# Edge rows added behind the column sums, and a third tile of re-read rows skipped by a branch

## The chip, the cores and the metric

The kernel runs on one core of one Trainium2 chip. The metric is the device time of that core in microseconds (us). Three runs of the kernel before gave a median of 324.0 us (323.58 to 324.59).

## What is computed

```python
N, d = feat.shape                      # 16384 rows of 256
q, k, v = feat @ Wq, feat @ Wk, feat @ Wv
starts = jnp.searchsorted(bids, jnp.arange(B))       # B = 8
pos = jnp.arange(N) - starts[bids]
qp, kp, vp = (pad(q), pad(k), pad(v))  # .at[bids, pos].set, LMAX = 3072 places each
scores = where(mask, einsum('bld,bmd->blm', qp, kp), NEG)
rp = einsum('blm,bmd->bld', softmax(scores), vp)
r = rp[bids, pos]
t = r @ Wt
mu, var = t.mean(axis=0), t.var(axis=0)
tn = (t - mu) / jnp.sqrt(var + EPS) * gamma + beta
return feat + relu(tn)
```

The segment numbers `bids` of the input are not sorted. So `pos` of many rows lies outside 0 to 3071. A row that is written to a place of its segment is an own row of it (436, 511, 542, 726, 701, 698, 431 and 468 rows in the eight segments). Rows whose `pos` runs past an end of the segment read the row at that end when results are fetched: these are the edge rows, two for each segment, 16 in all, and thousands of outputs use them. A further group of 199 rows writes a place that a later row overwrites, and reads back the other row's result: the kernel calls them losers, and keeps them in up to three tiles of 128 rows (LT = 3), the third of which is empty for this input.

The batch normalization at the end needs the sum and the sum of squares of each column over all 16384 rows of t, and then a scale and a shift for each column.

## The kernel before, in words

The kernel writes its instructions for five engines itself: TensorE (PE), VectorE (DVE), ScalarE (ACT), GpSimd (POOL) and SyncE (SP). A helper class records each operation (`op`, line 588), finds the operations that it depends on, and makes the engine wait on semaphores for them. Each engine runs its own operations in the order in which the code records them. Nothing reorders them later. So the order in the source text is the order on each engine.

The first part sorts the rows by segment. For each of eight segments e, POOL gathers the own rows into `xs`, in up to six tiles of 128 (FT = 6). PE and ACT form queries, keys and values, the scores and the exponentials. `attend(e, u)` (line 1273) multiplies the exponentials of tile u by the values on PE and takes a reciprocal on DVE; `scale` (line 1293) makes the result tile in `tk` and, after tiles 3 and 5, stores it to the table `t_rows` in device memory through SP's queue. Each result tile is then squared on ACT (`square`) and added to `acc` on DVE (`moments`, line 1337, two operations a tile), weighted by how often each row is read as an own row. In the last segment the tiles come in the order 0, 1, 4, 5, 2, 3.

The edge rows of the first seven segments are gathered from `t_rows` into `ecat` (line 1751). Edge rows that lie in the last segment are picked out of `tk` by small selection matmuls into `b_e`, a bank of PSUM: tiles 0, 4, 5 and 1 at line 1781, added to `ecat` at line 1786, squared at line 1787; tiles 2 and 3 at lines 1873 to 1875, added at line 1892 for the output alone (their share of the sums is in the weights `rw`).

Two matmuls close the column sums in the PSUM tile `sums`: one weighs the 16 edge rows and their squares (`we`, line 1876), one adds up the partitions of `acc` (line 1877). DVE transposes `sums` into `st_t` (line 1884), makes mean, variance, scale and shift, and transposes them back into `ss`.

The second part writes the output in 16 groups of 1024 rows. For a group, PE adds the edge row that each row reads (through the 0/1 matrices `hot`) into PSUM, and in some groups the input rows too (`open_group`). DVE (or ACT) brings the sum to the buffer `f`, and SP stores it. SP also loads the input rows for later groups, and counts each store that has landed in a semaphore `done`. Between the groups DVE normalizes the result tiles of one segment each (`normal`, `normal_more`). When a segment's groups have been stored, POOL scatters its tiles to their rows of the output, one indirect DMA for each 128 rows (`put`), because these rows must overwrite what the groups wrote. Behind the eight segments it scatters the three tiles `tl` of losers (line 2029). Tiles 4 and 5 of a segment are skipped by a branch where the segment has no such rows (line 2022). Last, POOL waits until all scatters have landed (a semaphore against a count in a register, loaded at line 1865) and all engines are through.

Of the kernel before, what the change touches and what calls it, by code (L numbers as in the profile page):

```python
# [11 lines left out]
I32 = mybir.dt.int32  # L12
BF16 = mybir.dt.bfloat16
F16 = mybir.dt.float16
AF = mybir.ActivationFunctionType
ALU = mybir.AluOpType
# [4 lines left out]
P = 128  # L21
NB = 8
# [8 lines left out]
LT = 3  # L31
# [870 lines left out]
def fast_path(nc, feat, bids, wq, wk, wv, wt, gamma, beta, out, bad):  # L902
    N, D = feat.shape
# [5 lines left out]
    NG = J // GT  # L909
    NL = NB + 1  # L910
    TT = NB * FT
    QA, QB = 4 * P, 2 * P
    pg = Fast(nc)

    room = ExitStack()
    start = nc._sbuf_addr_for_side("left")
# [9 lines left out]
    def new(name, shape, dtype=F32):  # L926
        nonlocal end
        size = mybir.dt.size(dtype)
        for d in shape[1:]:
            size *= d  # L930
        plan.append((name, shape, dtype, end))
        h = at(name, shape, dtype, end)
        end += size + -size % 32
        return h
# [30 lines left out]
    acc = new("acc", [P, 2, D])  # L965
# [4 lines left out]
    ecat = new("ecat", [P, 2, D])  # L970
# [17 lines left out]
    eidx, ridl, idxo = new("eidx", [P, 1], I32), new("ridl", [P, LT], I32), new("idxo", [P, LT], I32)  # L988
    eps_t = new("eps_t", [P, 1])
    armf, arm = new("armf", [1, NB]), new("arm", [1, NB], I32)  # L990
    upto, order = new("upto", [1, NB + 2], I32), new("order", [1, NG], I32)
    gb = new("gb", [P, 2, 32])
    gt_, bt_ = gb[:, 0, 0:NB], gb[:, 1, 0:NB]
    mq, ss8 = new("mq", [P, 2, NB]), new("ss8", [P, 2, NB])
# [75 lines left out]
    def load(eng, key, ap, hi, lo=0):  # L1070
        def emit(e):
            regs[key] = e.value_load(ap, min_val=lo, max_val=hi)

        pg.op(eng, emit, [ap], [], bare=True)
# [651 lines left out]
    for e in range(NB):  # L1726
# [18 lines left out]
        if last:  # L1745
            for u in (0, 1, 4, 5, 2, 3):
                step(e, u)
                if u == 0:
                    scores(e, 1, range(4))
                    late[2]()  # L1750
                    pg.gather(ecat[:, 0, :], t_rows[0 : (NB - 1) * FW, :], eidx[:], (NB - 1) * FW)
                    for g in range(FIRST, EARLY):
                        load_group(g)
                if u == 1:
                    scores(e, 1, range(4, 6))
                    late[4]()
                if u == 4:
                    late[3]()
                if u == 0:
                    lag[:0] = [(NB, t) for t in range(LT)]  # L1760
                if u == 5:
                    first = square(e, 1)
                    for g in range(EARLY, MID):
                        load_group(g)
                if u == 1:
                    pg.act(row_sum[:], ones[:], AF.Identity, scale=reads_r[:, e * FT + 1 : e * FT + 2])
                if u == 3:
                    any_ = hot[0 : 2 * NB, 0:2, :, :].rearrange("p k u x -> p (k u x)")
                    pg.mm(sums[:], none[0 : 2 * NB, :], any_, start=True, stop=False)
                    by_row(row_sum, first[0], first[2])  # L1770
                if u == 3:
                    while lag or squared:
                        if lag and len(squared) < 2:
                            squared.append(square(*lag.pop(0)))
                        else:
                            moments()
                else:
                    past(e)
                if u == 2:
                    b_e = ps_s[0]  # L1780
                    for u_ in (0, 4, 5, 1):
                        pg.mm(
                            b_e[:, 0:D], sel[:, u_, :], tk[:, e * FT + u_, :], start=(u_ == 0), stop=(u_ == 1),
                            pred=over4(e, u_),
                        )
                    pg.tt(ecat[:, 0, :], ecat[:, 0, :], b_e[:, 0:D], ALU.add)
                    pg.act(ecat[:, 1, :], ecat[:, 0, :], AF.Square)
        else:
            busy = e + 2 < NB
            step(e, 0, lambda: (xt_main(n, 0), xt_main(n, 1)))  # L1790
# [52 lines left out]
            if e == NB - 4:  # L1843
                prefix(NB - 1, NB)
                sizes(NB - 1)
                pg.copy("DVE", armf[:], arm[:])
                pg.red(cnt_f[0:1, 0:1], armf[:])
                pg.ts(upto[:, NB + 1 : NB + 2], cnt_f[0:1, 0:1], 16.0, ALU.mult, 16.0 * (4 * NB + LT), ALU.add)
                todo, late = rows()
                work.extend(todo)  # L1850
            scores(n, 0, range(4, 6))
# [2 lines left out]
            slot()  # L1854
        if last:
            assert not lag and not squared
        pg.end_region()
        if e == NB - 2:
            slot(99)
# [2 lines left out]
        load("POOL", ("g", e_), upto[0:1, e_ : e_ + 1], NG, 1)  # L1862
    for e_ in range(NB):
        load("POOL", ("t", e_), arm[0:1, e_ : e_ + 1], 2)
    load("POOL", "rows", upto[:, NB + 1 : NB + 2], 16 * (TT + LT), 16 * (4 * NB + LT))

    for g in range(MID, NF):
        load_group(g)
# [4 lines left out]
    b_e = ps_s[3]  # L1873
    for x, m in enumerate(last_two):
        pg.mm(b_e[:, 0:D], sel[:, 2 + x, :], tk[:, m, :], start=(x == 0), stop=(x == 1))
    pg.mm(sums[:], we[:], ecat[0 : 2 * NB, :, :].rearrange("p s d -> p (s d)"), start=False, stop=False)
    pg.mm(sums[:], ones[:], acc[:].rearrange("p s d -> p (s d)"), start=False, stop=True)
    pg.ts(good[:], rdens[:], LIM, ALU.is_lt)
    pg.stt(good[:], rdens[:], 1.0 / LIM, good[:], ALU.is_gt, ALU.mult, accum=odd[:])
    pg.ts(odd[:], odd[:], -1.0, ALU.mult, float(TT), ALU.add)  # L1880
# [145 lines left out]
            pg.op("POOL", emit, [idx[:, m : m + 1]], [])  # L2026
    look("POOL")
    pg.op("POOL", lambda x: (x.wait_ge(done, 1), x.wait_ge(done, regs[("g", NB)])), [], [])
    for t in range(LT):
        pg.put(out, idx[:, TT + t : TT + t + 1], tl[:, t, :], N)  # L2030

    held = pg.run("rows")
    held += [done, *row_done]
# [54 lines left out]
```

## Time and profile before

| | |
|---|---|
| median of three runs | 324.0 us |
| the profiled execution | 323.04 us |
| its span, first to last instruction | 318.4 us |
| busy: PE, DVE, ACT, POOL | 249.3, 238.8, 150.3, 133.8 us |
| mean granted TensorE clock | 0.866 |
| DMA over the span | 52.49 MB, 165 GB/s; 333 to 418 GB/s in most of the last third |
| chain that ended last, by engine | PE 41%, DVE 26%, ACT 11%, issue 9%, POOL 6%, DMA 4% |

The profile is of one execution. Times in it count from the span's start. A line of the chain or of a timeline gives the start, the duration, the engine, the line of code (often that of a helper: L803 is every matmul, L842 every scalar_tensor_tensor, L894 every unconditional scatter), and what is written from what. In brackets stands how long the engine was idle before it, and what ended that. A busy share is an average over the span; what a stage waits for is read from the stage's own lines. The sums are complete at 231.9 us, so the first part takes about 232 us and the second 86 us.

### The profile page before, as it was taken

What the parts mean: (1) busy time and instruction counts of PE and PEld (TensorE: products, weight loads), DVE (VectorE), ACT (ScalarE), POOL (GpSimd) and SP (SyncE); (2) the same over time, 40 slices, a digit from 0 to 9 for tenths busy, and PEclk for the clock granted to TensorE, in tenths of its full rate; (3) what the DMA queues carried; (4) which work ended last, traced back from release to release, by engine and by line L of the source; (5) the groups of instructions that cost most, each with busy time, mean ns of one, the idle gap of its engine ahead of it and who ended that gap; (6) DMA issues with size and microseconds to landing.
All of it is one profiled execution on the core that took longest, in us unless ns stands there. A gap on an engine that the chain in (4) does not pass through costs nothing.

```text
span 318.4 us, 4632 instructions
## 1 busy us (share of the span) xinstructions
PE 249.3 (78%) x1279; PEld 162.2 (51%) x1279; DVE 238.8 (75%) x773; ACT 150.3 (47%) x294; POOL 133.8 (42%) x143
## 2 busy tenths in 40 slices
PE   4699779998999999989999999859776955642600
PEld 2465547675676777667766777547322322210200
DVE  4845759988669576748776889866679999999930
ACT  3126949884764485255736557749501221111000
POOL 7433307051071034223502463776040337787873
PEclk9559979999999999999999999997965897775555
DMA  3101104114047014210300135198997999998795
GB/s 104 35 23 28 40 2 129 52 54 141 6 87 169 1 29 126 97 31 19 106 33 3 33 104 165 20 333 342 337 402 300 372 398 418 415 414 342 311 374 199
DMA packets 21533, 52.49 MB, mean 165 GB/s; under 512 B 5488, under 2 KB 14786, under 8 KB 17530
## 3 DMA queue, kind: packets, MB, share of 16 engines
q1 hardware_dynamic: 15674, 41.37, 34.6%
q0 software_dynamic: 5280, 10.18, 11.0%
q10 hardware_dynamic: 544, 0.52, 0.5%
q8 instruction: 15, 0.25, 0.3%
q14 instruction: 20, 0.16, 0.2%
HBM read 26.27 MB, written 28.74 MB: 173 GB/s over the span
## 4 chain that ended last, share of the span: by engine, by line
PE 41%; DVE 26%; ACT 11%; issue 9%; POOL 6%; DMA 4%; another core or an unknown queue 1%; POOLq 1%; DVEq 0%; SPq 0%
PE ps L803 39%; DVE tk L822 6%; DVE f L822 5%; POOL out L894 4%; ACT pa L813 4%; ACT xT L813 2%; PE ps L808 2%; DMA ecat<-t_rows,eidx 2%; ACT vs L818 2%; DMA t_rows<-tk 2%; DVE junk L829 2%; DVE k L819 1%; DVE tk L1942 1%; DVE tk L1944 1%; ACT xs L818 1%
## 5 line engine op out<-in xcount | busy, mean ns | idle before, releaser
L878 POOL DMA_INDIRECT xs<-in_r_feat,idx x48 | 50.8, 1059 | 100.3 <-DVE idx L842 52.0
L803 PE MATMUL ps<-vs,pa 128*128 128x257 f32 x312 | 78.0, 394 | 7.2 <-ACT vs L818 3.8
L803 PEld LDWEIGHTS ps<-vs,pa 128*128 128x128 f32 x312 | 57.9, 194 | 20.7 <-issue 7.5
L894 POOL DMA_INDIRECT out<-tk,idx x32 | 34.4, 1075 | 28.4 <-DVE tk L842 19.2
L803 PE MATMUL ps<-wvt,xT 128*128 128x256 f32 x156 | 37.5, 386 | 1.5 <-ACT vs L818 0.7
L818 ACT COPY f<-ps 128x1024 f32<-128x1024 f32 (+1 forms) x12 | 9.8, 835 | 58.7 <-PE ps L803 56.1
L803 PE MATMUL ps<-y,hot 32*128 32x256 bf16 x256 | 14.3, 353 | 26.5 <-DVE f L822 16.8
L803 PEld LDWEIGHTS ps<-wvt,xT 128*128 128x128 f32 x156 | 28.8, 190 | 11.3 <-ACT sq L813 2.3
L813 ACT ACTIVATE pa<-ps,mask 128x512 f32<-128x512 f32 x48 | 29.5, 687 | 10.6 <-PE ps L803 9.3
L803 PE MATMUL ps<-f,ident 128*128 128x512 f32 x38 | 29.0, 893 | 1.7 <-DVE f L822 1.2
L803 PEld LDWEIGHTS ps<-y,hot 32*128 32x128 bf16 x256 | 6.5, 111 | 43.6 <-DVE f L822 25.2
L822 DVE TENSOR_TENSOR f<-f,ps 128x1024 f32<-128x1024 f32 (+3 forms) x17 | 26.0, 1559 | 3.5 <-remote 2.9
L819 DVE COPY k<-ps 32x128 f32<-32x128 f32 x48 | 14.1, 294 | 17.5 <-PE ps L803 16.7
L818 ACT COPY vs<-ps 128x512 f32<-128x512 f32 x24 | 14.2, 590 | 25.2 <-PE ps L803 16.6
L813 ACT ACTIVATE q<-ps,cqk 96x512 f32<-96x512 f32 (+3 forms) x32 | 18.4, 573 | 13.6 <-PE ps L803 13.2
L855 DVE RECIPROCAL rdens<-ps 128x1 f32<-128x1 f32 x48 | 7.7, 160 | 22.6 <-PE ps L803 22.6
L803 PE MATMUL ps<-xT,w 128*128 128x512 f32 (+1 forms) x48 | 22.4, 593 | 2.3 <-ACT xT L813 2.3
L813 ACT ACTIVATE xT<-ps,negx 128x512 f32<-128x512 f32 (+1 forms) x32 | 17.0, 586 | 15.2 <-PE ps L808 9.8
L842 DVE SCALAR_TENSOR_TENSOR acc<-tk,reads_r,acc 128x256 f32<-128x256 f32 x45 | 21.4, 477 | 1.5 <-issue 1.3
L842 DVE SCALAR_TENSOR_TENSOR acc<-sq,reads_r,acc 128x256 f32<-128x256 f32 x45 | 21.5, 477 | 0.3 <-ACT sq L813 0.3
L878 POOL DMA_INDIRECT reads_r<-reads_of,idx x12 | 12.0, 1003 | 23.0 <-DVE ge L831 11.7
L813 ACT ACTIVATE pb<-ps,mask 128x256 f32<-128x256 f32 x48 | 19.3, 483 | 4.0 <-PE ps L803 3.8
(271 smaller groups left out, 426.2 us busy)
## 6 DMA issues: line engine op xcount, KB each, us to landing
f<-in_r_feat SPq DMA_DIRECT2D x16, 1024.0 KB, 7.7
out<-f SPq DMA_DIRECT2D x15, 1024.0 KB
t_rows<-tk SPq DMA_DIRECT2D x8, 512.0 KB, 4.2
t_rows<-tk SPq DMA_DIRECT2D x8, 256.0 KB, 2.2
eb<-edge_of SPq DMA_DIRECT2D x16, 64.0 KB
out<-f SPq DMA_DIRECT2D x2, 512.0 KB, 2.7
xs<-in_r_feat,idx POOLq DMA_INDIRECT x48, 3.6
out<-tk,idx POOLq DMA_INDIRECT x39
```

What stands on the lines that cost most here:

```text
L803: "PE", lambda e: e.matmul(out, lhsT, rhs, start=start, stop=stop, skip_group_check=True),
L808: return self.op("PE", lambda e: e.transpose(out, in_, ident), [in_, ident], [out], pred=pred)
L813: "ACT", lambda e: e.activation(out, in_, func, bias=bias, scale=scale), [in_, *more], [out]
L818: return self.op("ACT", lambda e: e.copy(out, in_), [in_], [out])
L819: return self.op(eng, lambda e: e.tensor_copy(out, in_), [in_], [out])
L822: return self.op(eng, lambda e: e.tensor_tensor(out, a, b, op), [a, b], [out])
L829: lambda e: e.tensor_scalar(out, a, s1, s2, op0, op1, accum_out=accum)
L842: else e.scalar_tensor_tensor(out, a, s, b, op0, op1),
L855: return self.op("DVE", lambda e: e.reciprocal(out, in_), [in_], [out])
L878: lambda e: e.indirect_dma_start(out=out, out_offset=None, in_=table, in_offset=bass.IndirectOffsetOnAxis(ap=ind, axis=0), bounds_check=n ...
L894: lambda e: e.indirect_dma_start(out=table, out_offset=bass.IndirectOffsetOnAxis(ap=ind, axis=0), in_=src, in_offset=None, bounds_check=n ...
L1942: v.tensor_tensor(y, y, scale, ALU.mult).then_inc(sem, 1)
```

## The change

Three things change. The add and the square of `ecat` move from behind the selection matmuls of tile 2 to the end of the last segment's loop, behind all operations that fill `acc`. The two matmuls that close `sums` change places. And the last of the three tiles of losers is scattered only if more than 256 rows are losers: DVE forms that flag and corrects the count of scatters to wait for (two more operations of one element each), POOL loads the flag into a register, and a branch passes over the scatter if it is 0.

```diff
-    upto, order = new("upto", [1, NB + 2], I32), new("order", [1, NG], I32)
+    upto, order = new("upto", [1, NB + 3], I32), new("order", [1, NG], I32)
...
                             pred=over4(e, u_),
                         )
-                    pg.tt(ecat[:, 0, :], ecat[:, 0, :], b_e[:, 0:D], ALU.add)
-                    pg.act(ecat[:, 1, :], ecat[:, 0, :], AF.Square)
...
                 pg.red(cnt_f[0:1, 0:1], armf[:])
-                pg.ts(upto[:, NB + 1 : NB + 2], cnt_f[0:1, 0:1], 16.0, ALU.mult, 16.0 * (4 * NB + LT), ALU.add)
+                lost = n_bc[0:1, NB : NB + 1]
+                pg.ts(upto[:, NB + 2 : NB + 3], lost, (LT - 1.0) * P, ALU.is_gt)
+                pg.stt(cnt_f[0:1, 0:1], lost, (LT - 1.0) * P, cnt_f[0:1, 0:1], ALU.is_gt, ALU.add)
+                pg.ts(upto[:, NB + 1 : NB + 2], cnt_f[0:1, 0:1], 16.0, ALU.mult, 16.0 * (4 * NB + LT - 1), ALU.add)
...
         if last:
             assert not lag and not squared
+            pg.tt(ecat[:, 0, :], ecat[:, 0, :], b_e[:, 0:D], ALU.add)
+            pg.act(ecat[:, 1, :], ecat[:, 0, :], AF.Square)
...
-    load("POOL", "rows", upto[:, NB + 1 : NB + 2], 16 * (TT + LT), 16 * (4 * NB + LT))
+    load("POOL", "rows", upto[:, NB + 1 : NB + 2], 16 * (TT + LT), 16 * (4 * NB + LT - 1))
+    load("POOL", "lost", upto[:, NB + 2 : NB + 3], 1)
...
-    pg.mm(sums[:], we[:], ecat[0 : 2 * NB, :, :].rearrange("p s d -> p (s d)"), start=False, stop=False)
-    pg.mm(sums[:], ones[:], acc[:].rearrange("p s d -> p (s d)"), start=False, stop=True)
+    pg.mm(sums[:], ones[:], acc[:].rearrange("p s d -> p (s d)"), start=False, stop=False)
+    pg.mm(sums[:], we[:], ecat[0 : 2 * NB, :, :].rearrange("p s d -> p (s d)"), start=False, stop=True)
...
-    for t in range(LT):
+    for t in range(LT - 1):
         pg.put(out, idx[:, TT + t : TT + t + 1], tl[:, t, :], N)
+
+    def put_last(x):
+        with x.If(regs["lost"] > 0):
+            pg.put_now(x, out, idx[:, TT + LT - 1 : TT + LT], tl[:, LT - 1, :], N)
+
+    pg.op("POOL", put_last, [idx[:, TT + LT - 1 : TT + LT], tl[:, LT - 1, :]], [])
```

## The prediction

> **What bounds the kernel now.** I read the chain of work that ended last, in order of time, because only what stands on it can shorten the span; then the timelines of DVE, PE and POOL around the two places that the change touches; then busy time by stretches; then the queue's own waits. The chain just ahead of the second half:
>
> ```profile
> 219.79 6.85 DMA ecat<-t_rows,eidx
> 226.66 0.43 DVE ecat L822
> 227.12 0.42 ACT ecat L813
> 227.54 0.37 ACT tk L813
> ...
> 227.95 3.94 PE ps L803 x6
> 231.91 0.73 DVE st_t L858
> ```
>
> The gather of the 16 edge rows lands at 226.66, and the in-order DVE stands in front of it. Behind DVE everything stops, as its timeline shows:
>
> ```profile
> 224.24 0.48 DVE L842 SCALAR_TENSOR_TENSOR acc<-sq,reads_r,acc 128x256 f32<-128x256 f32 x1
> 226.66 0.42 DVE L822 TENSOR_TENSOR ecat<-ecat,ps 128x256 f32<-128x256 f32 x1 [1.95 <-DMA ecat<-t_rows,eidx]
> 227.00 0.16 DVE L855 RECIPROCAL rdens<-ps 128x1 f32<-128x1 f32 x1
> ```
>
> and that of PE:
>
> ```profile
> 227.95 0.70 PE L803 MATMUL ps<-tk,sel 128*128 128x256 f32 x2 [1.96 <-ACT tk L813]
> 228.58 1.29 PE L803 MATMUL ps<-ecat,we 16*128 16x512 f32 x2
> 229.80 2.07 PE L803 MATMUL ps<-acc,ones 128*128 128x512 f32 x2
> ```
>
> The reciprocal at 227.00 belongs to the last attend, whose PE work ended at 224.2: it has nothing to do with the edge rows. From 231.91 (sums complete) DVE works through 239.15 to 299.4 almost without a gap, so the sums start the second half.
>
> The end of the chain is POOL, one scatter per 0.98 us busy plus 0.30 between:
>
> ```profile
> 310.52 0.98 POOL L894 DMA_INDIRECT out<-tl,idx  x1 [0.30 <-issue]
> 311.80 0.99 POOL L894 DMA_INDIRECT out<-tl,idx  x1 [0.30 <-issue]
> 313.10 0.98 POOL L894 DMA_INDIRECT out<-tl,idx  x1 [0.30 <-issue]
> ```
>
> In the trace's landing records the last scatter lands at 317.2, after which POOL closes (drain, clearing of semaphores) until 318.4. A second chain ends close by: SP's last counted store.
>
> ```profile
> L1953 SPq EVENT_SEMAPHORE x16: 17/17/28, 244.5 to 316.4; - x16
> ```
>
> POOL waits for both. So the end is bound by POOL with SP only 0.8 us behind.
>
> **Step 1: the ecat add leaves DVE's place ahead of the reciprocal.** In the new order DVE goes from the acc at 224.24 straight to the reciprocal. Neighbours in this run start 0.40 apart: 224.64. From its start to the end of the six acc operations behind it took 227.00 to 229.53 = 2.53, so acc is complete at 227.17 (it was 229.53). ACT must keep up: tk needs the reciprocal (224.80) and ACT, which is in a square until 225.18; tk 225.1 to 225.6, its square to 226.1; the sixth acc wants that at 226.7. It holds. The selection matmuls of the last tile follow the earlier ones on PE without the 1.96 gap, 225.84 to 226.3.
>
> The add itself now stands behind the six: start 227.1, and the data has been there since 226.66, so it waits for nothing; +0.42, ACT's Square to 227.97. Two edits of order follow: Square now stands behind tk and its square on ACT (no one waits), and ahead of ACT's table load (1.28 at 228.42), which then ends near 229.3; the Sqrt that needs it comes at about 231.2. Hidden, with 1.9 us of cover. The small DVE operations behind the add (good, odd, cnt_f, 0.7 together) end near 228.3, before the sums. Hidden.
>
> **Step 2: acc's matmul goes first, ecat's last.** acc can start at 227.2. Its price depends on PE's clock. The two passes of ecat in the trace started 0.53 apart (228.58, 229.11) at full clock, those of acc 1.01 apart (229.80, 230.81) at half; all are 512 columns. At full clock: 227.21 + 1.06 + 1.06 + 0.2 for the last pass to drain = 229.5; the ecat Square (227.97) is there when its turn comes at 228.27. At half clock: 227.21 + 2.02 + 2.02 + 0.2 = 231.45. Against 231.89 that is a gain of 2.3 or of 0.4.
>
> Which? Rows of the same trace, busy time by stretches (PE busy is the second number, PEclk the granted clock):
>
> ```profile
> 226.00:229.40 3.40, 1.45 (x4) 0.59 (x4) 2.73 (x8) 2.17 (x4) 0.00 (x0) 1.00 0.83 313
> 229.40:232.80 3.40, 3.40 (x6) 1.60 (x6) 1.52 (x8) 0.31 (x1) 0.00 (x0) 0.50 0.97 348
> 256.80:260.20 3.40, 2.48 (x20) 0.91 (x18) 3.33 (x3) 1.75 (x2) 0.00 (x0) 1.00 0.99 384
> ```
>
> A stretch with PE busy 1.45 of 3.4 (43%) was followed by half clock, one with 2.48 (73%) by full (1.00 from 260.2 to 263.5). In the new order PE idles only from 226.3 to 227.2, 0.9 of such a stretch: 73 to 74% busy. [...]
>
> Behind the sums one thing may be lost again: PE finishes the two early group matmuls sooner and may idle nearly 3 us until y is ready, so the 32 short matmuls ahead of the first group add (at full clock in the trace, from 236.2) can fall to half. Sixteen such took 0.61 at full and 1.04 at half, so the loss is 0 to 0.43. I take 0.4: gain at the first group add 2.3 - 0.4 = 1.9.
>
> **Step 3: does 1.9 us live to the end?** DVE is continuous from there, so its part moves along. POOL's first four scatters wait for DVE; the second four (260.88) in truth wait for SP's count of landed stores: DVE's second tk was done at 255.5, the fifth count came at 260.0. From there POOL is continuous. Store landings go over DMA engines that are full for a long time (DMA share is the number before GB/s):
>
> ```profile
> 239.00:245.00 6.00, 2.97 (x53) 1.24 (x41) 5.85 (x5) 1.07 (x2) 0.00 (x0) 0.55 0.68 272
> 245.00:291.00 46.00, 29.64 (x176) 10.54 (x176) 45.01 (x52) 7.80 (x9) 27.95 (x25) 0.76 1.00 400
> 291.00:301.00 10.00, 4.09 (x34) 1.40 (x34) 9.80 (x8) 0.36 (x1) 7.87 (x8) 0.50 0.74 288
> ```
>
> A full server can finish earlier only by closing earlier idle time: 32% of 6 us = 1.9 us lies between 239 and 245, and about 0.8 us between 223 and 232, where the t_rows store and three feat loads behind tk also issue some 2.3 us sooner. Together 2.7 us, more than 1.9. And from 291 to 301 the engines are at 0.74, so the last stores are paced by DVE again. I carry 1.9 through; the bounds are 0 and 2.3.
>
> **Step 4: the third scatter goes.** The segments lose 199 rows by the input's definition, under 256, so the branch is not taken. POOL ends 1.29 us earlier: last landing 317.2 - 1.3 = 315.9. SP's store (316.4) now comes last: of 1.29 only 0.8 counts. The skipped branch: between the scatters at 264.99 and 266.27 lie two branches not taken, and the gap is the 0.30 of all others; cost 0 to 0.15, taken as 0. The register load that feeds it is one more on POOL's sequencer; POOL waits 12.0 us there for t_rows. Two added one-element DVE operations (0.13 to 0.16 each, at 164.4): DVE idles 1.44 at 167.7 for PE, which waits for ACT; hidden, 0.3 if not. The sum of both parts: 1.9 + 0.8 = 2.7. The profiled execution took 323.0 (span 318.4, 4.6 around it): 320.3. The median of before is 324.0, 1.0 above it: 321.3.
>
> **The rivals.** *Clock at half* for acc and ecat: step 2 gives 0.4, with 0.8 of the scatter 1.2: 322.8. For it: the 73% is one example. Chance 0.14. *DMA absorbs it*: store landings hardly move, POOL's second four start where they did; only the scatter and some tenths remain: 323.1. For it: share 1.00 over 46 us. Against: the 2.7 us of idle ahead of it. Chance 0.14, on the line between faster and same. *Slower*: the earlier loads and stores crowd the DMA queue so that the fifth store lands later than before. It took 8.05 us from issue to count (251.97 to 260.02). POOL's 38 scatters behind that count have no slack; beyond the 1.3 of the scatter every further us moves the end, so it decides from a landing at 261.3; at 262.6 the end would be 1.3 later than before, 325.3. Against: the order of the queue is unchanged. Chance 0.10. That the branch does not skip would leave 1.9 and cost 0.8: 322.1, inside the range.
>
> **Numbers.** Forecast 0.62, alone 320.4 to 322.2. Faster by over 0.3% (about 1 us, what a measurement of this kernel can tell from no change): 0.62 + 0.14 + 0.05 = 0.81; same 0.09; slower 0.10. The range 320.2 to 323.6 leaves out the slower case and little else.
>
> **What would show it.** Reciprocal directly behind acc near 224.7 with no wait on ecat; acc's matmul before ecat's, passes 0.53 apart; sums read near 229.6; first group add near 237.3; POOL's second four near 259; two tl scatters; end within 1.3 of SP's last count. Wrong: acc's passes 1.01 apart (step 2), a gather that lands after 227.4 (the ecat matmul then waits), group adds earlier but POOL's second four still at 260.9 (step 3), or a pause like the unexplained 2.85 us ahead of DVE's last group add (306.16, "remote") in a new place.

## The result, and the profile after

| | before | after |
|---|---|---|
| median of 20 runs | 323.92 us (322.15 to 325.63) | 321.44 us (320.29 to 324.75) |
| the profiled execution | 323.04 us | 321.24 us |
| its span | 318.4 us | 316.4 us |
| reciprocal of the last attend | 227.00 | 224.80 |
| `acc` complete | 229.53 | 227.32 |
| sums read by DVE | 231.91 | 229.59 |
| first group add | 239.15 | 236.87 |
| POOL's fifth scatter of the half | 260.88 | 259.44 |
| last scatter issued, seen landed | 313.10, 317.21 | 310.94, 315.25 |
| SP's last counted store | 316.36 | 314.26 |

The ratio is 0.9942 with an interval of 0.992 to 0.9965, which is 1.9 us (1.1 to 2.6); the two medians lie 2.5 apart. Executions more than 1.5% above the fastest of their kernel are left out of all ratios here, not of the medians, and since the profiles of the branch alone and of the swap alone, further down, are of such executions, only their stretch up to the sums is read. The marks are in us from the start of the span of one profiled execution each.

The chain that ended last, around the sums, in order of time (start, duration, engine and what is written). The DMA and the `ecat` add are gone from it; it goes from DVE's last operations on `acc` straight to four PE passes:

```profile
226.44 0.88 DVE acc L842 x2
227.37 2.19 PE ps L803 x4
229.59 0.73 DVE st_t L858
```

DVE's timeline of the changed kernel at the same place. The reciprocal stands 0.40 behind the `acc` operation ahead of it, and no line has a bracket, so nothing is waited for. The add at 227.24 comes 0.5 behind the landing of the gather (226.74 here, from 219.89):

```profile
224.40 0.48 DVE L842 SCALAR_TENSOR_TENSOR acc<-sq,reads_r,acc 128x256 f32<-128x256 f32 x1
224.80 0.16 DVE L855 RECIPROCAL rdens<-ps 128x1 f32<-128x1 f32 x1
...
226.84 0.48 DVE L842 SCALAR_TENSOR_TENSOR acc<-sq,rw,acc 128x256 f32<-128x256 f32 x1
227.24 0.41 DVE L822 TENSOR_TENSOR ecat<-ecat,ps 128x256 f32<-128x256 f32 x1
```

PE's timeline. The idle gap shrank to 0.79, and the two passes of `acc` take 1.13 together where they took 2.07:

```profile
225.56 1.03 PE L803 MATMUL ps<-tk,sel 128*128 128x256 f32 x4
227.37 1.13 PE L803 MATMUL ps<-acc,ones 128*128 128x512 f32 x2 [0.79 <-DVE acc L842]
228.43 1.12 PE L803 MATMUL ps<-ecat,we 16*128 16x512 f32 x2
```

Busy time by stretches (the second number is PE busy, PEclk the granted clock, then the DMA share and GB/s). The clock is 1.00 in both stretches around the sums. The DMA engines, 0.68 busy in the six microseconds behind the first group add of before, are full in the like six of after:

```profile
226.00:229.40 3.40, 2.61 (x7) 0.77 (x5) 2.19 (x10) 1.91 (x3) 0.00 (x0) 1.00 0.90 233
229.40:232.80 3.40, 2.52 (x7) 0.82 (x6) 2.90 (x11) 0.30 (x1) 0.00 (x0) 1.00 1.01 389
...
236.90:242.90 6.00, 3.40 (x49) 1.42 (x42) 6.00 (x5) 1.17 (x2) 0.89 (x1) 0.50 1.00 409
```

POOL's timeline, at the start of the half and at its end. The fifth scatter now names SP's count as its releaser; two scatters of `tl` are left, with the same 0.30 between all:

```profile
253.33 0.98 POOL L894 DMA_INDIRECT out<-tk,idx  x1 [0.31 <-issue]
259.44 0.98 POOL L894 DMA_INDIRECT out<-tk,idx  x1 [5.13 <-SPq L1957]
260.73 1.72 POOL L894 DMA_INDIRECT out<-tk,idx  x1 [0.30 <-issue]
...
309.65 0.98 POOL L894 DMA_INDIRECT out<-tl,idx  x1 [0.30 <-issue]
310.94 0.99 POOL L894 DMA_INDIRECT out<-tl,idx  x1 [0.30 <-issue]
```

And SP's counted stores, the last at 314.3:

```profile
L1957 SPq EVENT_SEMAPHORE  x16: 17/17/28, 243.7 to 314.3; - x16
```

So the forecast's chain of steps is in the trace: 2.2 at the reciprocal, 2.3 at the sums and the first group add, 1.4 at the fifth scatter, 2.0 at the end. What the two traces leave open is which part is worth how much, and whether the 2.3 belongs to the change or to this execution of it.

### The profile page after: what moved, and what is told of

The parts are those of the page before. It is cut to its first block, busy times and chain, and to the rows that moved or that the text cites. A ratio compares the mean times of both kernels' runs of the same rounds, so it can differ in the third digit from the quotient of the medians.

```text
span 316.4 us, 4635 instructions
## 1 busy us (share of the span) xinstructions
PE 246.6 (78%) x1279; PEld 161.8 (51%) x1279; DVE 239.1 (76%) x775; ACT 150.7 (48%) x294; POOL 133.5 (42%) x142
## 4 chain that ended last, share of the span: by engine, by line
PE 43%; DVE 25%; ACT 13%; issue 9%; POOL 6%; another core or an unknown queue 2%; POOLq 0%; DVEq 0%
PE ps L803 40%; DVE tk L822 6%; DVE f L822 5%; ACT pa L813 4%; POOL out L894 4%; ACT xT L813 2%; ACT vs L818 2%; PE ps L808 2%; DVE acc L842 2%; DVE junk L829 1%; DVE tk L1946 1%; DVE tk L1948 1%; DVE k L819 1%; ACT xs L818 1%
## 5 line engine op out<-in xcount | busy, mean ns | idle before, releaser
L894 POOL DMA_INDIRECT out<-tk,idx x32 | 35.7, 1117 | 25.9 <-SPq L1957 17.4
L803 PE MATMUL ps<-y,hot 32*128 32x256 bf16 x256 | 15.1, 370 | 27.7 <-DVE f L822 19.1
L803 PE MATMUL ps<-f,ident 128*128 128x512 f32 x38 | 26.9, 831 | 2.0 <-DVE f L822 1.2
```

Source lines behind the costliest of these rows:

```text
L803: "PE", lambda e: e.matmul(out, lhsT, rhs, start=start, stop=stop, skip_group_check=True),
L894: lambda e: e.indirect_dma_start(out=table, out_offset=bass.IndirectOffsetOnAxis(ap=ind, axis=0), in_=src, in_offset=None, bounds_check=n ...
```

## The experiments

Twelve kernels ran in three groups, each on another chip and beside runs of the kernel before on that chip. Every ratio below is to those runs. The letters of the theories are explained in the expectations that use them. Each kernel has one profile, so what differs between two profiles can belong to the chip or the execution as well as to the edit.

| kernel | median, before on that chip (us) | ratio, interval |
|---|---|---|
| edge part alone | 324.15, 324.45 | 1.0008 [0.9974, 1.0043] |
| branch alone | 323.78, 324.45 | 0.996 [0.9928, 0.9992] |
| add moved, no swap | 325.94, 324.45 | 1.0047 [1.0018, 1.0076] |
| swap alone | 325.88, 324.45 | 1.0039 [1.0002, 1.0075] |
| before, PE kept busy in the gap | 324.75, 323.19 | 1.0021 [0.9988, 1.0055] |
| after, one more scatter dropped | 322.85, 323.19 | 0.9994 [0.9966, 1.0021] |
| after, PE's register read early | 323.39, 323.19 | 1.0025 [0.9992, 1.0058] |
| after, four matmuls behind the groups | 324.10, 323.19 | 1.0012 [0.9987, 1.0038] |
| after, again | 321.02, 321.89 | 0.9974 [0.9944, 1.0004] |
| before, gather issued late | 322.02, 321.89 | 0.9983 [0.9951, 1.0015] |
| after, gather issued late | 321.48, 321.89 | 0.9977 [0.994, 1.0014] |
| after, early loads moved | 321.44, 321.89 | 0.9988 [0.9958, 1.0018] |

### The edge part alone

The kernel before, with add and square at the end of the last segment's loop and the two matmuls swapped; three scatters of losers stay.

```diff
-                    pg.tt(ecat[:, 0, :], ecat[:, 0, :], b_e[:, 0:D], ALU.add)
-                    pg.act(ecat[:, 1, :], ecat[:, 0, :], AF.Square)
...
             assert not lag and not squared
+            pg.tt(ecat[:, 0, :], ecat[:, 0, :], b_e[:, 0:D], ALU.add)
+            pg.act(ecat[:, 1, :], ecat[:, 0, :], AF.Square)
...
-    pg.mm(sums[:], we[:], ecat[0 : 2 * NB, :, :].rearrange("p s d -> p (s d)"), start=False, stop=False)
-    pg.mm(sums[:], ones[:], acc[:].rearrange("p s d -> p (s d)"), start=False, stop=True)
+    pg.mm(sums[:], ones[:], acc[:].rearrange("p s d -> p (s d)"), start=False, stop=False)
+    pg.mm(sums[:], we[:], ecat[0 : 2 * NB, :, :].rearrange("p s d -> p (s d)"), start=False, stop=True)
```

> The edge part alone: the ecat add and square stand behind the acc operations and the two closing matmuls are swapped, but the third tile of losers is scattered as before. Theory A (the gather's wait left DVE's path, and the two parts add up at the end): sums read near 229.6 as in the changed kernel, first group add near 236.9, 42 scatters, the end about 1.3 us later than in the changed kernel, so 1.2 us under the kernel before (ratio 0.996). Rival C (only the skipped scatter counts, the DMA engines absorb the rest): sums at 229.6 but the end within 0.3 us of the kernel before. Rival D (the edge part alone is worth all of it, the scatter nothing): as the changed kernel, 2.5 us under.

Measured: 1.0008 [0.9974, 1.0043]: no gain, and one over 0.8 us is excluded. Its structure is the changed kernel's (`acc` passes 0.53 apart at a clock of 1.00, no wait on the gather), but everything stands 2.2 us later, and the sums are read at 231.75. DVE and then PE:

```profile
226.97 0.16 DVE L855 RECIPROCAL rdens<-ps 128x1 f32<-128x1 f32 x1
...
229.41 0.41 DVE L822 TENSOR_TENSOR ecat<-ecat,ps 128x256 f32<-128x256 f32 x1
```

```profile
229.54 1.12 PE L803 MATMUL ps<-acc,ones 128*128 128x512 f32 x2 [0.78 <-DVE acc L842]
230.60 1.12 PE L803 MATMUL ps<-ecat,we 16*128 16x512 f32 x2
```

The gather landed at 227.27 here. In the old order the add could not have started before 226.97, where the reciprocal stands, so it would have waited only 0.3. What makes it late lies further ahead, in a pause of PE, with which the third group deals.

### The branch alone

The kernel before, with the flag, the corrected count, the register and the branch; the edge part as it was.

```diff
...
-    for t in range(LT):
+    for t in range(LT - 1):
         pg.put(out, idx[:, TT + t : TT + t + 1], tl[:, t, :], N)
...
+    pg.op("POOL", put_last, [idx[:, TT + LT - 1 : TT + LT], tl[:, LT - 1, :]], [])
```

> The branch alone: the third tile of losers is passed over, the edge rows enter the sums as before. Theory A (POOL's end moves 1.29 us, but SP's last counted store stands 0.8 behind it): sums at 231.9, the end 0.8 us under the kernel before (ratio 0.9975), POOL waiting at the end for SP. Rival C: 1.3 us, if SP's store also comes earlier for want of the scatter. Rival D: nothing, ratio 1.000.

Measured: 0.996 [0.9928, 0.9992], a gain of 0.3 to 2.3 us, 1.3 by the ratio. It is the only part that gained in time when run alone, and the evidence is thin: the interval ends just under 1, and the medians are only 0.7 apart.

### The add moved without the swap

The first two pieces of the edge part's diff, not the third: `ecat`'s matmul still goes ahead of that of `acc`.

```diff
-                    pg.tt(ecat[:, 0, :], ecat[:, 0, :], b_e[:, 0:D], ALU.add)
-                    pg.act(ecat[:, 1, :], ecat[:, 0, :], AF.Square)
...
             assert not lag and not squared
+            pg.tt(ecat[:, 0, :], ecat[:, 0, :], b_e[:, 0:D], ALU.add)
+            pg.act(ecat[:, 1, :], ecat[:, 0, :], AF.Square)
```

> The ecat add and square stand behind the acc operations, but ecat's matmul is still issued before acc's, and all three tiles are scattered. Theory A (the swap lets acc's matmul cover the add and the square): PE waits for the square until about 228.1, then both matmuls at full clock, sums near 230.5, so 0.9 us later than with the swap: the end 0.3 to 0.5 us under the kernel before. Rival (the swap is worth nothing): the same as the edge part alone.

Measured: 1.0047 [1.0018, 1.0076], slower than before. PE's timeline has both costs. `ecat`'s matmul waits for ACT's square of the add that stands last on DVE, and behind that idle stretch the clock falls (at 232.4, behind a stretch with PE busy 1.83 of 3.4 at 1.00; 0.53 from 232.3 to 234.0), and `acc` takes 2.01 instead of 1.12:

```profile
228.65 1.03 PE L803 MATMUL ps<-tk,sel 128*128 128x256 f32 x4
231.24 1.12 PE L803 MATMUL ps<-ecat,we 16*128 16x512 f32 x2 [1.56 <-ACT ecat L813]
232.29 2.01 PE L803 MATMUL ps<-acc,ones 128*128 128x512 f32 x2
```

`acc` was complete at 230.41 and the sums were read at 234.34, 3.93 later; in the edge part with the swap it is 231.75 - 229.48 = 2.27. The swap is what makes the move harmless: 1.7 us, of which 0.9 is half clock (2.01 against 1.12).

### The swap without the move

```diff
-    pg.mm(sums[:], we[:], ecat[0 : 2 * NB, :, :].rearrange("p s d -> p (s d)"), start=False, stop=False)
-    pg.mm(sums[:], ones[:], acc[:].rearrange("p s d -> p (s d)"), start=False, stop=True)
+    pg.mm(sums[:], ones[:], acc[:].rearrange("p s d -> p (s d)"), start=False, stop=False)
+    pg.mm(sums[:], we[:], ecat[0 : 2 * NB, :, :].rearrange("p s d -> p (s d)"), start=False, stop=True)
```

> Only the two closing matmuls are swapped; the ecat add stays ahead of the reciprocal, three tiles are scattered. Theory A: acc is complete at 229.5 as before, then acc's and ecat's matmuls run one behind the other at half clock, 2.02 each, sums near 233.8: 1.9 us later than before, the end 1.5 to 2 us later than the kernel before (ratio 1.005). Rival (the place of the wait counts, not what stands behind it): within 0.3 us of the kernel before.

Measured: 1.0039 [1.0002, 1.0075]. DVE stands in the old order, and hardly waits for the gather, which landed at 226.71: the add comes 0.63 behind the start of the `acc` operation ahead of it, 0.23 more than neighbours need; in the profile of before it is 2.42 behind, 2.02 more. PE's clock was full without the move (1.00 from 222 to 234):

```profile
226.10 0.48 DVE L842 SCALAR_TENSOR_TENSOR acc<-sq,reads_r,acc 128x256 f32<-128x256 f32 x1
226.73 0.42 DVE L822 TENSOR_TENSOR ecat<-ecat,ps 128x256 f32<-128x256 f32 x1
227.07 0.16 DVE L855 RECIPROCAL rdens<-ps 128x1 f32<-128x1 f32 x1
```

```profile
229.64 1.12 PE L803 MATMUL ps<-acc,ones 128*128 128x512 f32 x2 [0.93 <-DVE acc L842]
230.70 1.12 PE L803 MATMUL ps<-ecat,we 16*128 16x512 f32 x2
```

The sums are read at 231.86, and at 231.75 in the edge part, where PE began its last attends 0.47 later (224.61 against 224.14): with the wait as short as this, moving the add is worth 0.1 as the lines stand, and some 0.6 from equal starts. Half clock, and with it the price put on the swap alone, did not come. Why its time lies above that of before (1.3 us by the ratio, interval 0.1 to 2.4) isn't shown.

### PE kept busy in the gap

The kernel before, with two matmuls of 512 columns into a bank not in use, ahead of the selection matmuls of the last tiles.

```diff
+    for _ in range(2):
+        pg.mm(ps_s[2][:], ones[:], tk[:, TT - FT : TT - FT + 2, :].rearrange("p t d -> p (t d)"))
     for x, m in enumerate(last_two):
```

> The kernel before with two more matmuls of 512 columns on PE in the gap that the late ecat add leaves there (225.8 to 227.9), into a bank that nothing uses; the output is not touched by them. It keeps PE busy, and leaves the wait of DVE as it is. Theory A (of the 2.3 us that the sums came earlier about 1 was the clock: acc's passes 1.01 apart at half against 0.53): the clock stays full from 229.4, acc's matmul takes 1.1, sums near 230.8: 1.0 to 1.1 us before the kernel before at that point, the end 0.5 to 1 us under it. Rival (the gap does not set the clock): half clock from 229.4 as before, sums near 231.9, no difference.

Measured: 1.0021 [0.9988, 1.0055]. The clock stayed full (1.00 from 222 to 234) and the passes of `acc` fell to 0.54, as in the changed kernel. But PE was late here (the pause again; DVE's wait for the gather was 0.30), and the added passes came at 227.11, where they stood in the way:

```profile
227.11 1.88 PE L803 MATMUL ps<-tk,ones 128*128 128x512 f32 x4
228.83 1.03 PE L803 MATMUL ps<-tk,sel 128*128 128x256 f32 x4
229.78 1.12 PE L803 MATMUL ps<-ecat,we 16*128 16x512 f32 x2
230.83 1.13 PE L803 MATMUL ps<-acc,ones 128*128 128x512 f32 x2
```

The sums are read at 232.00. For the time it is inconclusive, since the work added delayed the very matmuls that it was to speed up. For the clock too: the gap that was to be filled hardly existed here, and in the branch alone, which has the old order and no added matmuls, the passes of `acc` were 0.53 apart at full clock as well. The profile of before has a clock of 0.50 from 229.4, behind the gap of 1.96; that the gap was the cause is not shown by an experiment.

### One more scatter dropped

The changed kernel with one scatter of losers, and the count of scatters to wait for lowered by one; it leaves out the second tile of losers.

```diff
...
-    for t in range(LT - 1):
+    for t in range(LT - 2):
         pg.put(out, idx[:, TT + t : TT + t + 1], tl[:, t, :], N)
```

> The changed kernel without the second tile's scatter too; it leaves 71 rows of the output without their last value. Theory A (in the changed kernel POOL's last landing at 315.25 is still 0.9 us behind SP's last store at 314.3, so the branch's saving was fully used): the end 0.9 us earlier than in the changed kernel, SP last; ratio to the kernel before about 0.9895. Rival (the DMA engines or SP set the end): no difference from the changed kernel.

Measured: 0.9994 [0.9966, 1.0021]. POOL issues its last scatter 1.05 earlier than the next kernel on the same chip, which has both (a line of each):

```profile
311.55 0.98 POOL L894 DMA_INDIRECT out<-tl,idx  x1 [0.30 <-issue]
```

```profile
312.61 0.99 POOL L894 DMA_INDIRECT out<-tl,idx  x1 [0.30 <-issue]
```

But the last landing is seen at 316.77 against 316.89, and SP's last count is 316.26 against 316.03. The spans are 318.0 and 318.1. So in these two profiles POOL's issuing doesn't set the end: the last landing hardly follows it, and SP's last store ends within 0.9. By them a scatter dropped there is worth about 0.1 and not 0.9. The times can't exclude 0.9 (0.0028): this kernel's ratio is 0.0031 and 0.0018 below those of the two others of this group that hold the change, with intervals of some 0.003 to either side.

### The pause ahead of DVE's last group add

The prediction named a pause of 2.85 ahead of the last group add, put down to "remote". It stayed in the changed kernel (2.84). Two edits tried to reach it. The first reads PE's register early, so that no register load stands in PE's queue behind the last group:

```diff
+            load("PE", ("again", "PE"), bad[0:1, 0:1], P * TT + NL)
...
     for eng in ENGINES:
+        if eng == "PE":
+            continue
         load(eng, ("again", eng), bad[0:1, 0:1], P * TT + NL)
```

> The changed kernel with PE's register load of bad moved from behind the last group's matmuls to three groups earlier. It asks about the pause ahead of DVE's last group add (2.84 us in the changed kernel, 2.85 before), where the last matmul's semaphore came 3.3 us behind its modelled end. Theory P1 (the load on PE's sequencer holds the semaphore back): the pause goes, DVE's last add starts near 301.2, SP's last store lands up to 2.8 us earlier; the end moves only by what POOL leaves, 0 to 0.3 us. Theory P2 (the last matmuls are late for another reason, such as no matmul behind them): the pause stays at 2.8.

The second puts four matmuls behind the last group's:

```diff
+    for _ in range(4):
+        pg.mm(ps_m[1][:], ident[:], tk[:, 0:2, :].rearrange("p t d -> p (t d)"))
     again = {}
```

> The changed kernel with four more matmuls of 512 columns on PE behind the last group's, into a bank that nothing reads any more. Theory P2 (the completion of the last matmuls is reported late when no matmul follows): DVE's last add starts near 301.5 and the pause of 2.84 us is gone; the end moves 0 to 0.3 us, since POOL is last. Theory P1 (the register load behind them holds it back): the pause stays.

Measured: 1.0025 [0.9992, 1.0058] and 1.0012 [0.9987, 1.0038]. The pause is 4.42 in the first and 4.44 in the second, and 4.46 in the kernel with one more scatter dropped, which has neither edit. The line of the first:

```profile
307.25 2.29 DVE L822 TENSOR_TENSOR f<-f,ps 128x2048 f32<-128x2048 f32 x1 [4.42 <-remote]
```

Both explanations fall. In the next group there is no such pause: DVE's last four adds run for 7.81 without a gap, from 293.78 in the changed kernel run again and from 293.16 with the early loads moved. Note also that these two kernels and the one with a scatter fewer hold the whole change, and none of them was faster than the kernel before on this chip. The changed kernel itself was not run on it, so what their additions cost can't be taken off; the kernel with a scatter fewer adds nothing, and gained nothing.

### The changed kernel again, on a third chip

> The changed kernel once more, beside the kernel before on the same chip. In the eight runs so far PE ended the last attends 1.6 us later than in the first two profiles, so that the old order waits only 0 to 0.3 us for the gather there. Theory E (the edge part is worth what DVE waits for the gather, and that depends on when PE is done, behind a pause of its semaphore at 210 to 216): if the last reciprocal starts near 224.8, sums near 229.6 and the end about 2.3 us under the kernel before; if it starts near 226.4, sums near 231.2 and the end 0.8 to 1.2 us under. Rival F (the change is worth a fixed 2.5 us): 2.5 us under in either case.

Measured: 0.9974 [0.9944, 1.0004], 0.8 us by the ratio, against 0.9942 before. PE and DVE reached the end of the segment earlier than in any other profile (last reciprocal at 221.81), the gather landed at 225.27, and the add waited for it. `acc`'s passes were done by then, so only `ecat`'s matmul came behind: sums at 227.76, which is 2.49 behind the landing. The pause at the last group add was absent. The last scatter was issued at 307.88 and seen landed at 313.82, 5.9 later. Rival F, a fixed 2.5 us, falls: the interval ends at a gain of 1.8. That the gain is smaller on this chip than in the first result isn't shown by the times, since the two intervals overlap.

### The gather issued late, in both orders

If what the change saves is DVE's wait for the gather, then with equal landings of the gather the old order must lose to the new by a definite amount. Six small operations on POOL ahead of the gather move its issue; the same edit in the kernel before and in the changed one.

```diff
+                    for _ in range(6):
+                        pg.set("POOL", none[:], 0.0)
                     pg.gather(ecat[:, 0, :], t_rows[0 : (NB - 1) * FW, :], eidx[:], (NB - 1) * FW)
```

> The kernel before with six more small memsets on POOL ahead of the gather of the edge rows, so that it is issued and lands 1.2 to 1.8 us later; nothing else moves. Theory E: DVE stands before the ecat add until the gather has landed, so reciprocal, acc and sums come later by what the gather is late beyond 226.7: sums near 233.3 to 233.8, DVE idle 1.2 to 2 us before the add, the end about 1.3 us over the kernel before. Rival F (the wait is not what counts): sums near 231.9, no difference.

> The changed kernel with the same six memsets ahead of the gather. Theory E: reciprocal and acc do not see it; if acc ends at 228.9 as in the last runs the gather (landing 227.9 to 228.5) is still in time, sums near 231.2 as without it, 2 us or more ahead of the kernel before with the same late gather, the end 0.8 to 1.2 us under the kernel before. If acc ends at 227.3, the add waits for the gather: sums at its landing + 2.2. Rival F: the late gather costs here what it costs in the old order.

Measured: 0.9983 [0.9951, 1.0015] and 0.9977 [0.994, 1.0014], which tell nothing apart. The edit did less than it was meant to: issued 1.7 and 2.3 later than in the changed kernel on this chip, the gathers landed only 0.4 and 0.6 later (225.69 and 225.85). But the two landings lie within 0.16 of each other, so the traces can be compared. DVE with the old order, then with the new:

```profile
225.71 0.42 DVE L822 TENSOR_TENSOR ecat<-ecat,ps 128x256 f32<-128x256 f32 x1 [2.32 <-DMA ecat<-t_rows,eidx]
226.05 0.16 DVE L855 RECIPROCAL rdens<-ps 128x1 f32<-128x1 f32 x1
...
229.84 0.72 DVE L858 STREAM_TRANSPOSE st_t<-ps 128x512 f32<-128x512 f32 x1 [0.66 <-PE ps L803]
```

```profile
223.81 0.15 DVE L855 RECIPROCAL rdens<-ps 128x1 f32<-128x1 f32 x1
...
226.25 0.41 DVE L822 TENSOR_TENSOR ecat<-ecat,ps 128x256 f32<-128x256 f32 x1
...
228.60 0.72 DVE L858 STREAM_TRANSPOSE st_t<-ps 128x512 f32<-128x512 f32 x1 [1.33 <-PE ps L803]
```

The sums come 4.15 behind the landing in the old order and 2.75 in the new, the first group adds stand at 237.36 and 235.67, 1.7 apart. The lines also show the balance of the move. `acc` is complete at 228.57 and 226.32: the wait is gone, 2.25. But in the new order two matmuls are left then, in the old one only `acc`'s: sums 1.27 behind `acc` in the old order at a clock of 1.00, 2.28 in the new. So 2.25 - 1.01 = 1.24, the distance of the sums. (DVE came to this place 0.5 later in the new order's execution, 223.42 against 222.91 for the like `acc` operation; from equal starts it would be some 1.7.) In the profiles before and after, the old order's second part took 2.38 instead of 1.27, since `acc`'s passes ran at half clock (0.50): 2.21 + 0.11 = 2.32. So some 1.2 of the 2.3 there is DVE's wait beyond what the new order pays on PE, and 1.1 is the clock. The clock's part is the less certain: in all four other profiles in which the add stands ahead of the reciprocal, the passes of `acc` had full clock (the two took 1.12 in the swap alone and 1.13 with PE kept busy and here, and were 0.53 apart in the branch alone). Here DVE even waited longer, but PE, late itself, stood idle only 0.46.

By the same sum, as an estimate: without a wait the edge part takes the add's own 0.34 (226.66 to 227.00 in the profile of before) from the front of `acc` and puts 1.01 behind it. With a wait of 0.2 to 0.3 and full clock the sums would come some 0.4 later. That fits the edge part alone, which gained nothing.

### The early loads moved

A pause of PE at the head of the last segment bears on how long DVE waits. Its records stop between two groups of matmuls, and "issue" means that nothing shown is waited for. PE and ACT of the kernel before:

```profile
210.35 1.03 PE L803 MATMUL ps<-vs,pa 128*128 128x257 f32 x4
214.54 1.14 PE L803 MATMUL ps<-vs,pa 128*128 128x257 f32 x4 [3.16 <-issue]
```

```profile
213.90 0.58 ACT L818 COPY vs<-ps 128x512 f32<-128x512 f32 x1 [3.88 <-remote]
```

PE goes on when ACT's copy to `vs` is done, and in the first two groups the line of the pause names that copy. ACT had stood idle 3.88 us ahead of it, and 3.97 in the changed kernel, put down to "remote". What it waits for is a count of PE's own: here that came at 213.88, 2.5 behind the end of PE's last record. What held the count back is open. The pause ends at 214.54 here and at 214.71 in the changed kernel, but at 216.3 to 217.8 in all profiles of the first two groups. The last attends come that much later, and the gather doesn't: it landed at 226.5 to 227.3 in six of those eight. The edit takes two feature loads from the end of the last segment but one and issues them with the next three, in case their transfers cause the pause:

```diff
-                    for g in range(FIRST, EARLY):
+                    for g in range(1, EARLY):
...
-                load_group(1)
-                load_group(2)
```

> The changed kernel with the loads of groups 1 and 2 (2 MB) issued with the next three, about 10 us later, instead of at 205 to 207. It asks what holds PE's semaphore at 208 to 216, where no instruction that the profile shows is waited for. Theory S (the pause comes with the DMA traffic that starts there, 2 MB of loads beside the t_rows stores): the pause of 3.4 to 4 us shrinks to under 1, the last reciprocal starts 2 to 3 us earlier, the gather is issued and lands earlier too, the end 1.5 to 3 us under the changed kernel, unless the group loads then come late. Theory I (it has to do with PE's own stream of instructions): the pause stays, and the end is the changed kernel's.

Measured: 0.9988 [0.9958, 1.0018]. The pause is there, in another place, and its line names an ACT operation. ACT's lines lead on, to the gather of the loser tiles `tl`:

```profile
217.84 1.13 PE L803 MATMUL ps<-tk,sel 128*128 128x256 f32 x4 [3.71 <-ACT pb L813]
```

```profile
216.64 0.42 ACT L813 ACTIVATE sq<-tl 128x256 f32<-128x256 f32 x1 [3.54 <-DMA tl<-t_rows,ridl]
216.97 0.46 ACT L813 ACTIVATE tk<-ps,rdens 128x256 f32<-128x256 f32 x1
217.32 0.83 ACT L813 ACTIVATE pb<-ps,mask 128x256 f32<-128x256 f32 x2
```

The place is not the edit's doing. All four profiles of this group have the pause there, with the loads moved or not (1.36 in the changed kernel run again, 3.71 and 3.86 with the late gathers), and in all four ACT had waited for `tl` before. So on this chip the cause is in the lines: ACT stands in order before a square of `tl`, and what PE needs next stands behind it.

Nor does the run clear the loads. It issued all five from 209.07 to 211.7, where the changed kernel on this chip has two at 205.25 and three at 211.97, so all are still ahead of the pause. The first gather of `tl`, issued at 207.95, was used by DVE at 212.43; the second, issued at 209.25 behind the first of the loads, landed at 216.62. So the loads may well be what delays it on this chip; a run without loads there was not made. The gather of the edge rows landed at 224.23, 1.0 ahead of the changed kernel's on this chip, and nothing was gained at the end.

## Why the prediction was right, and where its sizes were off

The time was forecast as 321.3 and measured as 321.44. That it came so near is in part luck: the forecast took 2.7 us off 324.0, and the gain is 1.9 by the ratio and 1.8 between the two profiled executions. The main theory was that the move clears a wait of DVE and a loss of clock, and that a scatter fewer adds to it; its strongest rivals were half clock for `acc`, and DMA that absorbs it all.

**Step 1** held to 0.2: the reciprocal at 224.80 (224.64 forecast), `acc` complete at 227.32 (227.17), the add at 227.24 (227.1) without a wait.

**Step 2** held to 0.1: sums at 229.59 (229.5), at full clock. The rival of half clock did not come about here, nor in the passes of `acc` of any other kernel with the new order (the two took 1.12 in the edge part alone and with the late gather, 1.13 with PE's register read early). But the rows by which the step took full clock, 43% busy then 0.50 and 73% then 1.00, are no rule. Of the low shares, 54% in the kernel moved without the swap was followed by a clock of 0.53 and 64% in the changed kernel run again by 0.56, while 66% in the branch alone was followed by 1.00. High shares gave no safety: 77% from 226.0 was followed by 1.00 here, while in two other kernels with the new order the clock fell just after the sums, to 0.50 behind a stretch of 77% (PE's register read early) and to 0.51 behind one of 84% (late gather). The answer was right, and its margin thin. What half clock cost the old order, 1.1, stands in that one profile, and in none of the four others with the add in its old place.

Of the 0.4 set aside for the short matmuls ahead of the first group add, 0.2 was lost: from the first of them to the add it took 0.83 (236.04 to 236.87) where it had been 0.61 (238.54 to 239.15), since the clock fell at 236.2 (1.00 over the 3.4 us up to there, 0.52 from 236.0 to 240.0). What they wait for came 2.50 earlier, so the add gained 2.28, not 1.9.

**Step 3** carried "1.9 us through" to the end on the DMA's idle time. This is the mis-sized term, together with step 4. The first group add gained 2.28, POOL's fifth scatter only 1.44, since SP's count of landed stores, 260.02 before, came at 258.58. The DMA share went from 0.68 to 1.00 in the six microseconds behind the first group add, so the idle time was closed as the step says, but the store's landing got less of it. SP's last count moved 2.10, a little more than carried. So the rival that DMA absorbs it has a piece of the truth: 0.8 of 2.3 at the fifth scatter.

**Step 4** had POOL's end 1.29 earlier from the scatter alone and SP's store last. POOL's chain moved 1.44 at the fifth scatter and 2.16 at the last: 1.29 of that is the scatter, 0.87 is left of the move, because from the fifth to the last it took 0.57 longer per 36 scatters than before (51.50, against 52.22 - 1.29 = 50.93). The last landing came 1.96 earlier, and it is still behind SP's count (315.25 and 314.26), where the step had SP last. Steps 3 and 4 together put the last landing at 317.2 - 1.3 - 1.9 = 314.0. It came 1.2 later than that: 0.46 at the fifth scatter, 0.57 in the scatters behind it, 0.2 in the last landing. The dropped scatter of the second group points to what was overlooked: the last landing is not "issue plus a constant". There, 1.05 earlier issued moved it by 0.12; it came 4.1 to 5.9 us after its scatter's start in the profiles of before, after and after again.

The sum by the profiles is 2.0 of the span (1.8 of the execution's time) where 2.7 was forecast, and 1.9 by the ratio. Step 3's carry and step 4's scatter were each put at some tenths too much, and the first group add at some tenths too little.

**What the prediction could not see** is that step 1's 2.3 is no constant. It took DVE's wait of 1.95 from one profiled execution. On the chips of the first two groups the like wait was 0.2 to 1.1 in the profiles that had the old order, with PE's pause ending 1.7 to 3.2 later, and there the whole edge part, timed alone, gave 1.0008. The changed kernel gained 0.6% on the chip of the first result, 0.3% with an interval that reaches 1 on the third, and three kernels that hold it gained nothing on the second. So that DVE's wait for the gather holds up the sums, and that the new order takes it away, is shown in the traces. How much it saves goes with when PE is done and when the gather lands. The pause is not all of it: on the third chip the old order waited 2.32 (with the late gather), the sums stood 1.24 apart, and the changed kernel still gained only 0.8 us (-0.1 to 1.8). How much of what is gained at the sums reaches the end, and why it differs, is open; so is how much the scatter alone is worth (1.3 us with an interval of 0.3 to 2.3 on one chip, nothing seen from the next one on another). The slower rival, a fifth store that lands later, did not come about in the profile after: that store landed 1.44 earlier.

No version was found that clearly beats the changed kernel.

## What to carry to other kernels

Before a wait is priced, ask what decides when the engine arrives at it: if that is a pause or a stall elsewhere, the wait's length varies with it (here 1.95 in one profile, 0.2 to 1.1 in others), and so does the gain from moving the waiting instruction. Move a waiting instruction together with its consumer: with the `ecat` add moved and its matmul left in front, the wait only changed engines, and the kernel became slower by 0.5%. At an end like this one, with a DMA share of 1.01 from 301 to 310 in the profile of before, count landings and not issues: in one pair of profiles the last landing moved 0.1 us for a last issue 1.05 earlier.

## What was not expected of the hardware

- PE's records pause at the head of the last segment: for 3.16 us in the profile of before, 3.25 after, 3.66 with PE kept busy and 3.75 with the four matmuls, 1.36 to 3.86 on the third chip. There ACT had waited for the gather of `tl` (3.54 with the loads moved); in the profile of before ACT's copy waits for a count of PE's that comes 2.5 behind the end of PE's last record, and the cause is open. Ahead of the last group add there is a pause of 2.85 us before and 2.84 after, and of 4.42 to 4.46 in three profiles on the second chip; on the third the changed kernel has none. An earlier register load (4.42) and matmuls behind the last ones (4.44) did not remove it.
- The clock fell behind stretches in which PE was mostly busy. The late gather in the new order has the plainest case, in its stretches: 2.86 of 3.4 busy at 1.00, then a clock of 0.51.

```profile
225.60:229.00 3.40, 2.86 (x9) 1.10 (x8) 2.00 (x9) 1.70 (x2) 0.00 (x0) 1.00 0.90 226
229.00:232.50 3.50, 3.40 (x4) 0.51 (x3) 3.15 (x12) 0.30 (x1) 0.00 (x0) 0.51 1.02 394
```

- A gather issued 1.7 us later landed 0.4 later. From issue to landing it took 6.9 in the profile of before, with the DMA share at 0.92 to 0.99 in the 6 us from 222 to 228, and 4.1 and 3.7 with the late issue. What it spends this time on is not shown.
- Of the scatters on POOL, most take 0.98, and some 1.69 to 1.93: from the fifth of the half to the last there are four such in the profile of before, with one more of 1.56, and six after, where this stretch took 0.57 longer per 36 scatters.
